# A hybrid attention, state-space and spectral-filter kernel: the filter loop gets its own buffers, and its matrices and frequencies are dealt out by stride

## The chip, the cores and the metric

The kernel runs on one core of one Trainium2 chip, in float32. The metric is the time of one execution on the device in microseconds (us). A core has a matrix engine (TensorE, PE in the profile), VectorE (DVE), ScalarE (ACT), GpSimd (POOL) and SyncE (SP, which here issues nearly all DMAs, in order). TensorE reads its operands from SBUF and writes PSUM, 8 banks of 2 KB for each of 128 rows. "Eviction" means the copy of a PSUM result to SBUF by VectorE or ScalarE.

## What is computed

Input `x` is 8 images of 32 x 32 tokens with 128 channels. Three residual layers follow each other, softmax attention with 4 heads, a state-space layer run forward and backward, and a spectral filter over 1024 tokens an image:

```python
x = x + _L0_conv_ref(_gn(x), L0_conv_w_qkv, L0_conv_w_out, L0_conv_b_out)
t = _to_tokens(x)
t = t + _L1_attn_ref(_ln_t(t), L1_attn_fwd_in_proj, ...)
t = t + _L1_ffn_ref(_ln_t(t), L1_ffn_sigma, L1_ffn_phi, ...)
```

The change touches the last one. For tokens u, 16 filters phi and one of four banks of matrices, chosen by the weights:

```python
Vf = jnp.fft.rfft(phi, n=n, axis=0)
Uf_p = jnp.fft.rfft(u, n=n, axis=1)
Uf_m = jnp.fft.rfft(u * sgn3, n=n, axis=1)
U_plus = jnp.fft.irfft(Vf[None, :, :, None] * Uf_p[:, :, None, :], n=n, axis=1)[:, :sl]
U_minus = jnp.fft.irfft(Vf[None, :, :, None] * Uf_m[:, :, None, :], n=n, axis=1)[:, :sl]
out = jnp.einsum('btkd,k,kde->bte', U_plus, s, Mpp)
out = out + jnp.einsum('btkd,k,kde->bte', U_minus, s, Mpm)
```

To this comes a short regression over three shifted copies of u. The kernel does not filter and then multiply by the matrices; for each frequency it first sums the 16 matrices with the filters' spectra as weights, and then multiplies the token spectra by that one matrix.

## The kernel before

The part up to about 930 us (attention and most of the state-space layer) is not touched. Then come three stages, all inside `fast_kernel`:

1. *The end of the state-space stage* (lines 1448 to 1545), with all engines and SP in an order written by hand. Here batches 0 and 1 already get their token spectra, and the last lines add the state-space output to X[7], store it to `xd`, load it back in another layout (`reload(u)`, line 1542) and store the residual of batch 1 to `xa` (`store_residual(1)`).
2. *The spectra loop* (lines 1558 to 1625; b from 2 to 8). For each batch, `transform(b)` turns the normalized tokens (8 transposes `cpt`, line 561), forms their spectra (16 matmuls `pf`, line 571; the additions that finish them run on VectorE and GpSimd), stores them to DRAM (`store_spectra`, to `ud`, 1 MB) and copies the turned tokens to `ut`. `taps_of(b - 1, k)` does the regression of the batch before (matmuls `pu`, line 601, in two halves) and adds it to X; then X goes to `xa`. Between the halves, in b = 2 to 5, `turned(n)` takes a quarter (bank) of the 32 matrices from DRAM (`md`, eight matrices in a row), transposes them (`mdt`, line 1573), copies them to `me` in SBUF (line 1574) and stores them to DRAM `me` (line 1577). After the fourth bank, four DMAs of 512 KB (line 1580) spread all of `me` into `mst`: 32 rows for each of four groups, a row for each matrix.
3. *The filter loop* (lines 1629 to 1744). The 128 frequencies go in 16 chunks of 8. For a chunk, `matrices(c, n, gs)` is called for n = 0 to 7: 16 small matmuls `pg` (line 1644) into four one-bank PSUM tiles, evicted in turn by ScalarE (line 1657) and VectorE (line 1655) to `gs`, 64 KB a row. `loaded_spectra(c)` brings the chunk's spectra `u` from `ud` and GpSimd makes a second, turned copy (lines 1667 and 1668). `apply` multiplies (`py`, line 1678), `gather` combines the results and stores them to `yd` (line 1701). Chunk c + 1 gets its matrices while chunk c is applied, two calls and one quarter of `apply` in alternation; the first chunk's matrices come alone. `fetch(c)` (line 1709) brings a part of chunk c's results back as rows of `early_yt`. After the loop the rest is loaded (line 1753), and the inverse transform `pz` (line 1769) and the last additions give the output.

In the spectra loop PE, DVE, ACT and POOL keep the program's order and SP's order is the scheduler's; in the filter loop likewise. Buffers come from pools that are opened and closed as a stack, on two sides of SBUF. The filter loop's pool `g_2` holds two `gs` and two `u`; it opens where the spectra loop's pools and the pool `resid` with all X[b] have just been closed (`middle.close()`), so it lies on the places that these had. Whoever first writes such a place waits for all that still uses it. The PSUM pools change at the same point: in the spectra loop `ps_f` has two tiles of two banks, `ps_o` two of one, `ps_t` one of two; in the filter loop `ps_g` has eight of one.

Of the kernel before, what the change touches and what calls it, by code (L numbers as in the profile page):

```python
# [14 lines left out]
P = 128  # L15
B = 8
# [29 lines left out]
def fast_kernel(ctx: ExitStack, tc: tile.TileContext, a: dict, out: bass.AP, bad: bass.AP):  # L46
# [29 lines left out]
    me = dram.tile([P, 2 * KF, P], F32, name="me")  # L76
# [243 lines left out]
    def transforms(pool, tables):  # L320
# [5 lines left out]
        odd = counted(pool, [2, NF], [[512, 2], [2, NF]], 1, 0, "odd")  # L326
# [31 lines left out]
    def transform_taps(pool, ps, tables):  # L358
# [34 lines left out]
        alt = pool.tile([P, NF // 2, 2], F32, name="alt")  # L393
        nc.gpsimd.memset(alt, 1.0)
        nc.gpsimd.memset(alt[:, :, 1], -1.0)
        alt = alt.rearrange("p f i -> p (f i)")
# [533 lines left out]
    with ExitStack() as s:  # L930
# [611 lines left out]
        reload(u)  # L1542
# [10 lines left out]
    with ExitStack() as s:  # L1553
        mp = s.enter_context(tc.tile_pool(name="c_m", bufs=1, side="right"))
        mst = mp.tile([P, 32, C], F32, tag="mst", name="mst")
        early_yt = mp.tile([P, 2, 4, 4, C], F32, name="early_yt")

        with ExitStack() as s2:
            p1 = s2.enter_context(tc.tile_pool(name="f_1", bufs=1))
            p2 = s2.enter_context(tc.tile_pool(name="f_2", bufs=2))  # L1560
            ps_f = s2.enter_context(tc.tile_pool(name="f_ps_f", bufs=2, space=PSUM))
# [3 lines left out]
            def turned(n, pool, tag, size):  # L1565

                t = p2.tile([P, 8, C], F32, tag="md", name=f"md{n}")
                nc.sync.dma_start(t, md.rearrange("d r k e -> d (r k) e")[:, n * 8 : n * 8 + 8, :])
                to = p2.tile([P, 8, C], F32, tag="me", name=f"me{n}")
                for at in range(0, 8, size):  # L1570
                    pt = pool.tile([P, size, C], F32, tag=tag, name=f"mdt{n}_{at}")
                    for i in range(size):
                        nc.tensor.transpose(pt[:, i, :], t[:, at + i, :], ident)  # L1573
                    nc.vector.tensor_copy(
                        to[:, at : at + size].rearrange("p k d -> p (k d)"), pt.rearrange("p k d -> p (k d)")
                    )
                nc.sync.dma_start(me[:, n * 8 : n * 8 + 8, :], to)
                if n == 3:
                    for g in range(4):
                        nc.sync.dma_start(  # L1580
                            mst[g * 32 : (g + 1) * 32],
                            me[g * 32 : (g + 1) * 32].rearrange("n k d -> k n d"),
                        )
# [23 lines left out]
            s2.enter_context(tc.manual_schedule(engines=IN_ORDER))  # L1607
            uts = {}
            for _ in scaled(3, *third, p2):
                pass  # L1610
            for b in range(2, B + 1):
                if b + 2 < B:
                    norms[b + 2] = normalize(p2, b + 2)
                if b < B:
                    transform(b)
                if 3 < b + 1 < B:
                    for _ in normalized(b + 1, p2, *norms.pop(b + 1), wide=p2):
                        pass
                if b > 2:
                    taps_of(b - 1, 0)  # L1620
                if 2 <= b <= 5:
                    turned(b - 2, *((ps_o, "o", 4) if b == 2 else (ps_t, "t", 8)))
                if b > 2:
                    taps_of(b - 1, 1)
                    store_residual(b - 1)
        middle.close()
        middle.close()

        with ExitStack() as s2:
            p2 = s2.enter_context(tc.tile_pool(name="g_2", bufs=2))  # L1630
            p3 = s2.enter_context(tc.tile_pool(name="g_3", bufs=3))
            ps_g = s2.enter_context(tc.tile_pool(name="g_ps_g", bufs=8, space=PSUM))

            turn = 0

            def matrices(c, n, gs):

                nonlocal turn
                pts = [ps_g.tile([P, 4, P], F32, tag="g", name=f"pg{c}_{n}_{g}") for g in range(4)]
                cols = slice(c * FC, (c + 1) * FC)  # L1640
                for e in range(4):
                    for g in range(4):
# [948 lines left out]
```

## Time and profile before

| what | value |
|---|---|
| median of 3 runs | 1395.06 us (1393.53, 1395.06, 1397.17) |
| profiled execution, its own time | 1403.45 us |
| its span, first to last instruction | 1401.6 us |
| mean granted TensorE clock | 0.980 |
| TensorE busy | 1330.1 us, 95% of the span |
| VectorE, ScalarE, GpSimd busy | 79%, 66%, 38% |
| spectra loop | about 999 to 1069 us |
| entry to the filter loop (no `py` yet) | 1069 to 1088 us |
| filter loop with `py` | 1088 to 1356 us |
| tail | 1357 to 1402 us |

A row of the timeline reads: start in the span, duration, engine, line, operation, tile written <- tiles read, shapes, count of instructions merged; in brackets the time that the engine sat idle before it, and what released it. "SPq" is the issue of a DMA by SP; its duration is that of the issue, not of the transfer. "issue" as a releaser means that the engine waited for nothing that the profile shows. The granted clock is TensorE's, as a share of full speed.

In the filter loop with `py` TensorE is busy for 246.5 of 252.4 us (stretch 1088.4 to 1340.8), at clock 1.00 and a DMA share of 0.27.

### The profile page before, as it was taken

To read this page: it belongs to the slowest core of one execution; us is meant where nothing else is said; L and a number is where in the kernel's file an instruction comes from. 1 tells how busy PE (TensorE), PEld (TensorE's weight loads), DVE (VectorE), ACT (ScalarE), POOL (GpSimd) and SP (SyncE) were. 2 spreads that over 40 slices of the span, in tenths; PEclk is the share of its full clock that TensorE was granted. 3 is DMA by queue.
4 is the path that set the end of the run, shared out by engine and by line. 5 is a ranking of instruction groups with operands and counts; after the bars stand their busy time and mean duration, and the time that the engine had idled before them with its cause. 6 is when DMAs were issued, how large, how long until landed. Compare 5 with 4: busy or idle time off the path is not lost. (4 is left out here: it accounts for less than half of the span.)

```text
span 1401.6 us, 47569 instructions
## 1 busy us (share of the span) xinstructions
PE 1330.1 (95%) x20926; PEld 844.7 (60%) x20926; DVE 1103.4 (79%) x2145; ACT 922.8 (66%) x1428; POOL 536.0 (38%) x510
## 2 busy tenths in 40 slices
PE   7999999999999999999999999998898999999967
PEld 4333333333333666666666666667797988888964
DVE  5789888788778688988889898999564777777745
ACT  5666666766756888888878888876353555555520
POOL 3412986876910343434343343444673011111100
PEclk9999999999999999999999999999999999999979
DMA  7100111111101434444444343431668132222357
GB/s 172 55 2 2 38 39 39 53 39 39 31 1 42 96 78 93 108 94 113 94 108 94 92 95 88 114 83 48 197 208 198 46 78 73 77 69 70 83 171 294
DMA packets 139391, 123.24 MB, mean 88 GB/s; under 512 B 44808, under 2 KB 118152, under 8 KB 135080
## 3 DMA queue, kind: packets, MB, share of 16 engines
q1 hardware_dynamic: 137048, 115.93, 32.0%
q8 instruction: 166, 2.72, 0.8%
q10 hardware_dynamic: 2128, 4.19, 0.8%
q14 instruction: 49, 0.40, 0.1%
HBM read 78.15 MB, written 34.08 MB: 80 GB/s over the span
## 5 line engine op out<-in xcount | busy, mean ns | idle before, releaser
L809 ACT ACTIVATE pr<-pt 128x1024 f32<-128x1024 f32 x256 | 248.2, 1022 | 105.0 <-PE pt L804 103.9
L1657 ACT COPY gs<-pg 128x512 f32<-128x512 f32 x256 | 133.1, 603 | 75.6 <-PE pg L1644 58.4
L1655 DVE COPY gs<-pg 128x512 f32<-128x512 f32 x256 | 159.1, 685 | 26.0 <-PE pg L1644 18.9
L834 DVE TENSOR_TENSOR two<-pr,pr 128x1024 f32<-128x1024 f32 x128 | 164.8, 1328 | 15.2 <-ACT pr L809 15.2
L804 PE MATMUL pt<-q,k 32*128 32x512 f32 x1024 | 162.5, 651 | 6.1 <-ACT pr L809 4.1
L1644 PE MATMUL pg<-taps,mst 32*128 32x128 f32 x4096 | 150.1, 283 | 11.9 <-issue 5.8
L1644 PEld LDWEIGHTS pg<-taps,mst 32*128 32x128 f32 x4096 | 135.0, 189 | 27.2 <-issue 19.3
L825 PE MATMUL po<-pr,v 128*32 128x512 f32 x1024 | 140.6, 610 | 0.0
L1678 PE MATMUL py<-gs,u 128*32 128x128 f32 (+1 forms) x4096 | 130.9, 281 | 3.4 <-issue 3.4
L1030 POOL TENSOR_TENSOR ec<-ec,ct 128x2048 f32<-128x2048 f32 x16 | 83.6, 5224 | 112.3 <-ACT ct L1110 57.1
L1072 DVE SCALAR_TENSOR_TENSOR xs<-xp,cw,xs 128x1024 f32<-128x1024 f32 x96 | 122.5, 1283 | 2.2 <-issue 0.2
L1678 PEld LDWEIGHTS py<-gs,u 128*32 128x32 f32 (+1 forms) x4096 | 114.8, 141 | 10.9 <-issue 3.6
L1094 PE MATMUL pb<-bxt,wbc 128*128 128x512 f32 x256 | 114.0, 597 | 3.6 <-ACT zs L1085 3.6
L1667 POOL TENSOR_SCALAR u<-u 128x512 f32<-128x512 f32 x16 | 24.0, 1499 | 237.5 <-DMA u<-ud 138.3
L804 PEld LDWEIGHTS pt<-q,k 32*128 32x128 f32 x1024 | 49.5, 185 | 88.9 <-ACT pr L809 27.1
L1193 DVE SCALAR_TENSOR_TENSOR state<-state,dec,pst 128x64 f32<-128x64 f32 x448 | 87.3, 275 | 1.1
L1302 POOL TENSOR_TENSOR rms<-rms_v,mhalf 128x8 f32<-128x8 f32 x16 | 26.5, 1659 | 157.0 <-DVE rms_v L1300 157.0
L1094 PEld LDWEIGHTS pb<-bxt,wbc 128*128 128x128 f32 x256 | 47.1, 189 | 60.3 <-issue 55.0
L825 PEld LDWEIGHTS po<-pr,v 128*32 128x32 f32 x1024 | 27.8, 110 | 89.7 <-issue 86.4
L1016 POOL TENSOR_TENSOR lm<-cs,lm 128x2048 f32<-128x2048 f32 x16 | 57.9, 3620 | 57.7 <-DVE xs L1072 22.6
L845 PE MATMUL pd<-two,ones 128*32 128x512 f32 x512 | 74.1, 618 | 2.3 <-DVE two L834 2.1
L1272 PEld LDWEIGHTS spo<-wo,y 128*128 128x128 f32 x512 | 62.1, 191 | 13.1 <-issue 8.9
(310 smaller groups left out, 2784.5 us busy)
## 6 DMA issues: line engine op xcount, KB each, us to landing
lm<-cd SPq DMA_DIRECT2D x32, 512.0 KB
ec<-cd SPq DMA_DIRECT2D x32, 512.0 KB
ud<-sp SPq DMA_DIRECT2D x8, 1024.0 KB
u<-ud SPq DMA_DIRECT2D x32, 256.0 KB
yd<-sums SPq DMA_DIRECT2D x32, 256.0 KB
moved<-state SPq DMA_DIRECT2D x48, 128.0 KB
room<-yd SPq DMA_DIRECT2D x6, 1024.0 KB
X<-in_x SPq DMA_DIRECT2D x8, 512.0 KB
```

The costliest lines, as they stand in the source:

```text
L804: nc.tensor.matmul(pt[:, i, :], lhsT=k[rows, j * P : (j + 1) * P], rhs=q[rows, cols], start=True, stop=True)
L809: nc.scalar.activation(pr[:, 2 * g : 2 * g + 2, :].rearrange("p i t -> p (i t)"), pt.rearrange("p i t -> p (i t)"), AF.Exp, scale=SCALE,)
L825: nc.tensor.matmul(po[rows, :], lhsT=vs[b][:, j, rows], rhs=pr[:, h, :], start=(j == 0), stop=(j == NT - 1))
L834: nc.vector.tensor_tensor(two, sums["pr"][:, 2 * g : 2 * g + 2, :], pr[:, 2 * g : 2 * g + 2, :], ALU.add)
L1030: t = nc.gpsimd.tensor_tensor(u.ec, u.ec, u.ct.unsqueeze(1).to_broadcast([P, NH, NT, L]), ALU.mult)
L1072: u.convolved = nc.vector.scalar_tensor_tensor(acc, xp[:, at : at + T], cw[u.d][:, n, i : i + 1], acc, ALU.mult, ALU.add)
L1094: nc.tensor.matmul(u.pb[:, i * 512 : (i + 1) * 512], lhsT=wbc[u.d][:, k, :], rhs=xt[:, at : at + 512], start=(k == 0), stop=(k == KC - 1),)
L1193: nc.vector.scalar_tensor_tensor(u.state[:, k, h, :], u.state[:, k - 1, h, :], u.dec[:, c, h, j : j + 1], u.pst[c][:, j, h, :], ALU.mult, ...
L1644: nc.tensor.matmul(pts[g][:, e, :], lhsT=mst[rows, n * 4 + e, :], rhs=taps[rows, cols].rearrange("p f q m i -> p (f q m i)"), start=True, ...
L1655: nc.vector.tensor_copy(to, frm)
L1657: nc.scalar.copy(to, frm)
L1678: nc.tensor.matmul(py[t * 32 : t * 32 + 32 - 16 * m, q // 2, :], lhsT=u[:, i, m:, :, :, q * FC + f].rearrange("p k b i -> p (k b i)"), rhs ...
```

## The change

- The matrices are dealt out by stride. `me` is laid out as four banks of eight; bank n takes the matrices n, n + 4, n + 8 and so on, so it is loaded from `md` in runs of 512 bytes. Each bank is spread to `mst` by four DMAs of its own, `spread(n)`, at the start of b = 4, 5, 6 and 7: 8 rows each, every fourth row of a group. So 16 DMAs of 128 KB take the place of 4 of 512 KB.
- `turned(n)` moves from b = 2 to 5 to b = 3 to 6. All banks have buffers from a pool of three (`f_m`); banks 0 to 2 are asked for ahead of the loop, bank 3 in `turned(0)`. The first bank no longer uses the half-size PSUM tiles of `ps_o`.
- `reload(u)` of X[7] moves behind the load of bank 0; with that, `store_residual(1)` stands ahead of it on SP. SP is in hand-written order in the spectra loop.
- `gs` and `u` of even chunks come from a pool `c_g` that opens ahead of the spectra loop, on the other side of SBUF; those of odd chunks from a pool `g_g` on the old place. `early_yt` is taken later.
- Two of the eight calls of `matrices` for chunk 0 move into the last pass of the spectra loop (b = 8), one between the two halves of batch 7's regression, one after them, with two `ps_f` tiles each. `u` of chunk 0 is loaded at the end of that loop.
- Chunk c now has the frequencies c, c + 16, c + 32, ...: the tables `odd` and `alt` are permuted, `yd` is written four separate frequencies at a time, and `fetch` fills rows of `early_yt` that are 16 apart.

```diff
-    me = dram.tile([P, 2 * KF, P], F32, name="me")
+    me = dram.tile([P, 4, KF // 2, P], F32, name="me")
...
-        odd = counted(pool, [2, NF], [[512, 2], [2, NF]], 1, 0, "odd")
+        odd = counted(pool, [2, NF // FC, FC], [[512, 2], [2, NF // FC], [2 * NF // FC, FC]], 1, 0, "odd")
+        odd = odd.rearrange("p i c f -> p i (c f)")
...
-        alt = pool.tile([P, NF // 2, 2], F32, name="alt")
+        alt = pool.tile([P, NF // FC // 2, 2, FC], F32, name="alt")
...
         add_rows(u)
-        reload(u)
         for k in range(NB):
             add_taps(1, k, po[:, k])
         store_residual(1)
...
-        early_yt = mp.tile([P, 2, 4, 4, C], F32, name="early_yt")
+        first_gs = s.enter_context(tc.tile_pool(name="c_g", bufs=1, side="right"))
...
-                t = p2.tile([P, 8, C], F32, tag="md", name=f"md{n}")
-                nc.sync.dma_start(t, md.rearrange("d r k e -> d (r k) e")[:, n * 8 : n * 8 + 8, :])
+            def load_bank(n):
+                mds[n] = pm.tile([P, 8, C], F32, tag="md", name=f"md{n}")
+                nc.sync.dma_start(mds[n], md.rearrange("d r k e -> d (r k) e")[:, n::4, :])
+
+            def turned(n):
+
+                if n == 0:
+                    load_bank(3)
+                pt = ps_t.tile([P, 8, C], F32, tag="t", name=f"mdt{n}")
+                for i in range(8):
+                    nc.tensor.transpose(pt[:, i, :], mds[n][:, i, :], ident)
                 to = p2.tile([P, 8, C], F32, tag="me", name=f"me{n}")
...
-                nc.sync.dma_start(me[:, n * 8 : n * 8 + 8, :], to)
-                if n == 3:
-                    for g in range(4):
-                        nc.sync.dma_start(
-                            mst[g * 32 : (g + 1) * 32],
-                            me[g * 32 : (g + 1) * 32].rearrange("n k d -> k n d"),
-                        )
+                nc.vector.tensor_copy(to.rearrange("p k d -> p (k d)"), pt.rearrange("p k d -> p (k d)"))
+                nc.sync.dma_start(me[:, n], to)
+
+            def spread(n):
+                for g in range(4):
+                    nc.sync.dma_start(
+                        mst[g * 32 + n : (g + 1) * 32 : 4],
+                        me[g * 32 : (g + 1) * 32, n].rearrange("n k d -> k n d"),
+                    )
...
-            s2.enter_context(tc.manual_schedule(engines=IN_ORDER))
-            uts = {}
-            for _ in scaled(3, *third, p2):
+            s2.enter_context(tc.manual_schedule(engines=ALL_IN_ORDER))
+            uts, mds = {}, {}
+            for n in range(3):
+                load_bank(n)
+                if n == 0:
+                    reload(units[-1])
+            gs, begun = {0: chunk_matrices(0, first_gs)}, set()
+
+            def double_banks(n):
+                pts = [ps_f.tile([P, 2, 4, P], F32, tag="f", name=f"pg0_{n}_{i}") for i in range(2)]
+                begun.add((-1, n))
+                matrices(0, n, gs[0], [pts[g // 2][:, g % 2] for g in range(4)])
+
+            def ahead(b, place):
+                for _ in range(planned.get((b, place), 0)):
+                    double_banks(len(begun))
+
+            planned = {(B, 1): 1, (B, 2): 1}
+            for _ in scaled(3, *third, px):
                 pass
             for b in range(2, B + 1):
+                if 4 <= b <= 7:
+                    spread(b - 4)
...
+                ahead(b, 0)
                 if b > 2:
                     taps_of(b - 1, 0)
-                if 2 <= b <= 5:
-                    turned(b - 2, *((ps_o, "o", 4) if b == 2 else (ps_t, "t", 8)))
+                ahead(b, 1)
+                if 3 <= b <= 6:
+                    turned(b - 3)
                 if b > 2:
                     taps_of(b - 1, 1)
                     store_residual(b - 1)
+                ahead(b, 2)
+            us = {0: loaded_spectra(0, first_gs)}
...
+            second_gs = s2.enter_context(tc.tile_pool(name="g_g", bufs=1))
+            yp = s2.enter_context(tc.tile_pool(name="g_y", bufs=1, side="right"))
+            early_yt = yp.tile([P, 2, 4, 4, C], F32, name="early_yt")
...
-                at = c * FC + n * 4
+                at = c + n * 4 * chunks
                 nc.sync.dma_start(
-                    yd[at : at + 4].rearrange("f k b i q e -> (f k b i) (q e)"), sums.rearrange("p q e -> p (q e)")
+                    yd[at :: chunks][:4].rearrange("f k b i q e -> f (k b i) (q e)"), sums.rearrange("p q e -> p (q e)")
                 )
...
-                rows = slice(c * FC, (c + 1) * FC)
+                rows = slice(c, NF, chunks)
...
                 if c + 1 < chunks:
-                    gs[c + 1] = p2.tile([P, P, C], F32, tag="gs", name=f"gs{c + 1}")
-                    us[c + 1] = loaded_spectra(c + 1)
+                    if c >= 0:
+                        gs[c + 1] = chunk_matrices(c + 1, second_gs if c % 2 == 0 else first_gs)
+                        us[c + 1] = loaded_spectra(c + 1, second_gs if c % 2 == 0 else first_gs)
...
-                        matrices(c + 1, 2 * n, gs[c + 1])
-                        matrices(c + 1, 2 * n + 1, gs[c + 1])
+                        for i in range(2 * n, 2 * n + 2):
+                            if (c, i) not in begun:
+                                matrices(c + 1, i, gs[c + 1], single_banks(c + 1, i))
```

## The prediction

> **What bounds the kernel now.** I read the page's busy shares first, then the table of stretches, then the chain of waits in order of time and the timeline around each pause of TensorE. TensorE is busy for 95% of the span, so only its pauses, its slow stretches and the tail can be won. The change touches what lies after about 999 us. From the table of stretches, spectra loop and filter loop (columns: start:end, length, busy time of each engine with the number of instructions, granted TensorE clock, DMA share, GB/s):
>
> ```profile
> 995.00:1010.00 15.00, 9.17 (x58) 8.22 (x57) 7.32 (x25) 5.34 (x12) 11.38 (x21) 0.90 0.70 204
> 1010.00:1022.50 12.50, 12.50 (x82) 11.73 (x81) 7.39 (x24) 5.34 (x12) 8.02 (x15) 0.84 0.65 218
> 1022.50:1033.10 10.60, 10.60 (x83) 10.19 (x82) 7.76 (x24) 5.34 (x12) 7.52 (x15) 1.00 0.76 249
> ...
> 1069.00:1088.40 19.40, 14.02 (x320) 13.51 (x320) 11.21 (x19) 9.54 (x19) 4.08 (x4) 0.82 0.54 141
> ```
>
> The second and third lines are the same work for two batches: 12.5 us at clock 0.84, 10.6 at 1.00. Two pauses stand before the slow lines. Timeline, with the idle time of the engine and its releaser in brackets:
>
> ```profile
> 1003.40 1.09 ACT L566 COPY ut<-cpt 128x512 f32<-128x512 f32 x2
> 1008.00 1.94 PE L1573 MATMUL mdt<-ident,md 128*128 128x128 f32 x8 [5.11 <-DMA md<-md]
> 1009.73 1.91 PE L561 MATMUL cpt<-ident,ln_x 128*128 128x128 f32 x8
> ...
> 1044.13 0.37 SPq L592 DMA_DIRECT2D ud<-sp  x1
> 1044.61 1.81 SPq L1577 DMA_DIRECT2D me<-me  x1
> 1050.90 4.57 SPq L1580 DMA_DIRECT2D mst<-me  x4
> ...
> 1069.22 2.07 PE L1644 MATMUL pg<-taps,mst 32*128 32x128 f32 x64 [0.84 <-DVE X L611]
> 1075.81 2.05 ACT L1657 COPY gs<-pg 128x512 f32<-128x512 f32 x4 [16.49 <-DMA xa<-X]
> 1075.92 2.49 DVE L1655 COPY gs<-pg 128x512 f32<-128x512 f32 x4 [6.75 <-DMA xa<-X]
> 1082.42 7.27 DVE L1655 COPY gs<-pg 128x512 f32<-128x512 f32 x12 [0.42 <-PE pg L1644]
> 1088.43 2.02 PE L1678 MATMUL py<-gs,u 128*32 128x128 f32 x64
> ```
>
> The first pause is a wait for the first turned bank, 5.11 us. The second: eight PSUM banks are full after 2.07 us, and no eviction may start because `gs0` lies where X[7] is still being stored. The chain of waits shows that store, and at the end of the loop two transfers that stand on the path:
>
> ```profile
> 1069.60 5.75 DMA xa<-X
> ...
> 1357.57 2.40 DMA yd<-sums
> 1359.99 3.53 DMA early_yt<-yd
> ```
>
> **What the Trainium skill says.** (1) "DMA: Bandwidth & Descriptors", section "Why a DMA increments its semaphore by 16 and not by 1": a DMA runs on the largest number of engines up to 16 that divides the outermost sizes of both sides. The new spreads have 8 rows, the new `yd` stores have 4 on one side, so 8 and 4 engines where 16 worked. No row of before shows such a store. (2) "SBUF — State Buffer", section "Door 1: The DMA port swizzle (why `[64,N]` ≈ `[32,N]`)": 32 rows in a row reach half the ports, 189 GB/s at 1 MiB. The trace agrees: the spread of `mst` filled 1052 to 1063 at 188 GB/s. (3) "TensorE: Matmul & The Clock Gate", Part 1: after some 3.4 us of idleness the clock halves until about 3.4 us of work have passed. The trace agrees: a pause of over 5 us stands before each of the stretches at 0.84 and 0.82, and 1009 to 1011 shows 0.50.
>
> **Part one, start of the spectra loop.** `turned(0)` moves from batch 2 to batch 3, its bank is asked for before the loop, and store_residual(1) now stands between bank 0 and the reload of X[7]. The next TensorE work after 1002.9 is then transform(3), which needs the two copies of `ut`, done at 1004.49, and `ln_x`, done earlier. It starts near 1004.6, not 1009.73: -5.1 us. Batch 3 then runs warm: from its first transpose to batch 4's took 12.8 us (1009.73 to 1022.53), the two batches after it 10.56 each; I take 10.6, so -2.2 (ends 0 and -2.2). Bank 0 must be there at 1004.6 + 0.87 + 3.46 + 2.68 = 1011.6; in 512-byte pieces it takes 1.9 us (0.52 MB at 281 GB/s, the rate of the `ud` stores in 1023 to 1027, whose runs are 512 bytes), behind `ud` and `xd` at about 1009.5: covered. `turned(3)` now stands in batch 6, which had none: 8 transposes, +0.9. Sum -6.4. VectorE loses two half copies of 0.69 and gains a whole one of 1.22; GpSimd needs some 8 us of each 10.6: both hidden.
>
> **Part two, entry to the filter loop.** Before: from the last `pu` (1068.38) to the first `py` (1088.43) 20.05 us. After, `gs0` has a place of its own, so the store of X[7] holds nothing until `gs1`. The built program gives this order on TensorE: pu(7,0), a call of matrices, pu(7,1), a second call, six more. A call is 1.04 us (half of 2.07). The two early calls share PSUM tiles in pairs, and the built waits show VectorE's eviction held until ScalarE's of the same tile is done, and call three held until VectorE's last: 0.59 + 0.68 + 0.68 + about 0.1 = 2.1 us. Then 1.04 for call three and twelve evictions on VectorE. The pace is from before: sixteen took 1075.92 to 1082.42 + 8 x 0.606 = 1087.27, 0.71 each; twelve, 8.5. From the sixteenth to `py` 1.16. Sum, leaving out pu(7,1), which both have: 1.04 + 1.04 + 2.1 + 1.04 + 8.5 + 1.16 = 14.9, so -5.2, less a wait s.
>
> The wait s is what the change adds: the early calls read every fourth matrix of all four spreads, and pu(7,1), the store of X[7] and `u0` stand behind them. The last spread: batch 6 starts at 1004.6 + 3 x 10.6 = 1036.4; `ud` of a batch is issued 11.05 us after it (1033.09 to 1044.13), so 1047.4; from there to the landing of `me` was 6.8 us (1044.13 to 1050.90), so SP issues the spread at 1054.2. With 8 engines at 281/16 GB/s, 141 GB/s, it takes 3.7 us, plus about 1 us at each end (taken from the last `xa`: the DMA share fell to 0.24 in 1073 to 1074 and 0.06 in 1074 to 1075, ScalarE went on at 1075.81): 1059.9. It is needed at 1047.0 + 0.87 + 3.46 + 5.36 + 2.68 = 1059.4. But the queue is nearly full: from 999 to 1059 six `ud` of 3.7, eleven half-megabyte transfers of 1.3 (400 GB/s in 1049 to 1051), four banks of 1.9 and four spreads of 3.7 make 58.9 us of 60, with SP standing in order before each spread for its `me`. The idle half of the engines during a spread helps. I take s = 1.5, ends 0 and 5. Part two: -3.7.
>
> Hidden here: sixteen spread issues on SP in place of four (some 0.8 us each, covered by the engines' 10.6 us per batch; where not, that is s); `u0`, issued after the store of X[7] near 1066 and ready 7.6 us later as before (1075.61 to 1083.2), some 4 us ahead of `py`; `gs1`'s wait for the same store, landed near 1068, used near 1077.
>
> **Part three, loop and tail.** In the loop the `yd` stores on 4 engines take about 2.6 us each where 0.65 did (0.26 MB at 400 GB/s, times 16/4); two to a chunk of 16.5 us, at a DMA share of 0.30: hidden. The last store is on the path: +2.0 (ends 0 and 2). The fetch to rows sixteen apart reaches four ports where eight rows in a row reach two (place 2 above); the two fetches of 1109.0 to 1110.5 ran at 98 GB/s, so I take -0.8 (ends 0 and -1). Net +1.2. The permuted tables (`odd`, `alt`) have equal sizes: nothing.
>
> **Sum.** -6.4 - 3.7 + 1.2 = -8.9 us. On the profiled execution of 1403.45 us (span 1401.6 and 1.85 around it) that is 1394.5. It was 8.4 us above the median of the three runs, 1395.06; I carry the difference over: 1386.2. The ends together: best -6.4 - 5.2 - 1 = -12.6, worst -4.2 - 0.2 + 2 = -2.4, so 1382.5 to 1392.7; the runs scatter by 1.8 around the middle.
>
> **Rivals.** *Late spreads*: the wait moves from X[7] to `mst`, s of 5 to 8. For it: the count of 58.9 of 60 us; against it: spreads fill gaps in which the queue stood still (a DMA share of 0.01 in 1019 to 1022). Then about -3.5: 1391.5. *The entry stays as long*: some other wait (evictions held in pairs, `u0`, `gs1`) takes all of part two. For it: each of the first twelve evictions has a new companion; against it: each wait is shorter than the 5.75 us it replaces. Then -6.4 + 1.2 = -5.2: 1389.9. *Spreads so slow that the kernel is slower*: four in series on one in-order queue, so each further microsecond of a spread is paid four times. With s = 1.5 + 4 x (spread - 3.7) the gain is gone at s = 10.4 (5.9 us a spread) and the kernel is slower by over 4 us from 7.0 us a spread, 75 GB/s. At 7.5 us, s = 16.7 and the change is +6.3: 1401.4. For it: half the engines, each with one row; against it: 141 GB/s by the same packets elsewhere. *The change doesn't do what it says* (bank 0 still late) gives back the 7.3 of part one: -1.6, 1393.5, counted with late spreads.
>
> **How the numbers follow.** Forecast 0.70, late spreads 0.15, entry as long 0.09, slower 0.06. A difference of 0.3%, 4.2 us, is about what a measurement of this kernel tells from no change. Faster by more (below 1390.9): nearly all of the first, 0.4 of the second, 0.7 of the third: 0.81; slower 0.06; the same 0.13. Range: the ends, the scatter, and most of the second case: 1381.5 to 1392.5.
>
> **What would show it.** Right: no TensorE pause over 2 us near 1003; 1.00 in the stretch of batch 3; the first `py` near 1079; a pause of 0 to 5 us before the first `pg`, released by `mst`; a last `yd` store of over 4 us in the chain. Wrong: a longer pause before `pg`, transposes of batch 3 waiting for `md`, or `py` still near 1088.

## The result, and the profile after

The changed kernel takes 1400.1 us (median of 22 runs, 1392.97 to 1405.22), the kernel before, run beside it, 1398.21 us (22 runs, 1392.96 to 1403.21). The ratio is 1.0012 with a 95% interval of 0.9999 to 1.0025: no change, or up to 3.5 us slower. Forecast were 8.9 us less. The profiled execution has a span of 1398.5 us at a mean clock of 0.984 (before: 1401.6 at 0.980); it took 1400.27 us, close to its kernel's median.

The table of stretches of the changed kernel, for the places that were shown of before (start:end, length, busy time of PE, PEld, DVE, ACT and POOL with instructions, granted TensorE clock, DMA share, GB/s):

```profile
995.00:1010.00 15.00, 12.62 (x83) 11.30 (x83) 9.93 (x42) 6.55 (x17) 11.91 (x22) 1.00 0.63 180
1010.00:1022.50 12.50, 12.50 (x97) 12.03 (x96) 8.96 (x27) 6.58 (x15) 11.59 (x23) 1.00 0.86 261
1022.50:1033.10 10.60, 10.60 (x82) 10.19 (x82) 7.81 (x25) 5.37 (x13) 8.02 (x16) 1.00 0.76 241
...
1055.00:1069.00 14.00, 10.24 (x86) 9.05 (x85) 2.25 (x3) 0.58 (x2) 3.75 (x8) 0.85 0.82 270
```

The clock of 0.84 behind 1010 is gone: the start of the spectra loop runs warm. The low clock and the idle TensorE stand now in 1055 to 1069, which was at 1.00 before. The timeline of the changed kernel shows why:

```profile
1006.05 1.09 PE L562 MATMUL cpt<-ident,ln_x 128*128 128x128 f32 x8 [1.66 <-ACT ut L567]
...
1049.83 2.80 SPq L1622 DMA_DIRECT2D mst<-me  x4
1052.74 0.41 SPq L593 DMA_DIRECT2D ud<-sp  x1
1053.25 3.48 SPq L1618 DMA_DIRECT2D me<-me  x1
...
1060.47 2.80 SPq L1622 DMA_DIRECT2D mst<-me  x4
1063.39 0.48 PE L1581 MATMUL pg<-taps,mst 32*128 32x128 f32 x2 [2.51 <-DMA mst<-me]
...
1064.96 3.82 PE L1581 MATMUL pg<-taps,mst 32*128 32x128 f32 x30 [1.09 <-DMA mst<-me]
1068.70 4.26 PE L602 MATMUL pu<-m_u,ut 128*128 128x128 f32 x24
...
1085.71 2.02 PE L1711 MATMUL py<-gs,u 128*32 128x128 f32 x64
```

Read SP's lines first. The four transfers that spread bank 2 are issued at 1049.83, because SP stood there for bank 2's store (`me`) to land; only then come `ud` and, at 1053.25, the store of bank 3. That store has to land before bank 3's own spread, which is issued at 1060.47. Batch 7 began at 1048.35, so the last spread is issued 12.1 us after it. TensorE has reached the first early call of `matrices` (tile `pg`) near 1060.9 and waits, first 2.51 us, then in shorter pieces; the second half of the last regression, which stands behind this call, starts at 1068.70 and takes 4.26 us for 24 matmuls where 2.84 are usual. The tail of the changed kernel:

```profile
1349.40 0.54 SPq L1734 DMA_DIRECT2D yd<-sums  x1
1349.98 6.93 SPq L1742 DMA_DIRECT2D early_yt<-yd  x3
1356.96 2.34 SPq L1788 DMA_DIRECT2D gs<-yd  x4
1358.33 5.31 PE L1804 MATMUL pz<-early_yt,inv 128*128 128x512 f32 x8 [10.24 <-DMA early_yt<-yd]
...
1384.20 1.67 PE L1804 MATMUL pz<-gs,inv 128*128 128x256 f32 x6 [2.96 <-SPq L2596]
```

The same place before, where the last store was issued at 1357.57:

```profile
1357.94 2.67 SPq L1709 DMA_DIRECT2D early_yt<-yd  x3
1360.66 2.22 SPq L1753 DMA_DIRECT2D room<-yd  x4
1363.87 6.18 PE L1769 MATMUL pz<-early_yt,inv 128*128 128x512 f32 x8 [7.60 <-DMA early_yt<-yd]
```

SP stood with the fetches for 6.93 us (2.67 before), since they wait for the last `yd` store. The loads of the other three quarters (`gs<-yd`, before `room<-yd`) stand behind them in the same queue: they are issued 7.56 us after the last store instead of 3.09. At 1384.20 TensorE goes on after another pause, of 2.96 us. It is put down to line 2596 on SP, the branch on a flag at the end of the program, which these matmuls do not need. The matmuls behind the pause read the last of these loads, and the kernel with the dealing alone names that load (below, "The tail").

### The profile page after: what moved, and what is told of

Read it like the earlier page. It is cut to its first block, busy times and chain, and to the rows that moved or that the text cites. A ratio compares the mean times of both kernels' runs of the same rounds, so it can differ in the third digit from the quotient of the medians.

```text
span 1398.5 us, 47581 instructions
## 1 busy us (share of the span) xinstructions
PE 1325.5 (95%) x20926; PEld 841.6 (60%) x20926; DVE 1105.9 (79%) x2144; ACT 922.0 (66%) x1428; POOL 537.4 (38%) x510
## 5 line engine op out<-in xcount | busy, mean ns | idle before, releaser
L835 DVE TENSOR_TENSOR two<-pr,pr 128x1024 f32<-128x1024 f32 x128 | 164.1, 1322 | 13.4 <-ACT pr L810 13.0
L805 PEld LDWEIGHTS pt<-q,k 32*128 32x128 f32 x1024 | 49.5, 185 | 88.3 <-ACT pr L810 27.0
L1017 POOL TENSOR_TENSOR lm<-cs,lm 128x2048 f32<-128x2048 f32 x16 | 57.9, 3620 | 57.7 <-DVE xs L1073 34.7
```

What stands on the lines that cost most here:

```text
L805: nc.tensor.matmul(pt[:, i, :], lhsT=k[rows, j * P : (j + 1) * P], rhs=q[rows, cols], start=True, stop=True)
L835: nc.vector.tensor_tensor(two, sums["pr"][:, 2 * g : 2 * g + 2, :], pr[:, 2 * g : 2 * g + 2, :], ALU.add)
```

## The experiments

Every kernel was timed in five rounds beside the kernel before (the one repeat of before in one round), and profiled once. All ratios are to the kernel before, as it ran in the same rounds. Where two edited kernels are compared by their ratios, the difference is uncertain by some 3 us, an estimate from the widths of the two intervals. The stretches are differences of starts in the timelines: from the first `cpt` of batch 2 to that of batch 7 (start of the spectra loop), from there to the first `py` (entry), and from the last chunk's first `py` to the end (tail), in us.

| kernel | start | entry | tail | ratio (95%) |
|---|---|---|---|---|
| before | 55.7 | 35.3 | 60.8 | 1 |
| before, profiled again | 55.5 | 35.2 | 58.4 | 0.9991 (0.9972 to 1.0010) |
| changed | 49.4 | 37.4 | 63.1 | 1.0012 (0.9999 to 1.0025) |
| before, banks ahead | 49.4 | 40.5 | 58.8 | 1.0009 (0.9986 to 1.0033) |
| ... last two banks in batch 5, one after the other | 51.0 | 35.1 | 58.8 | 0.9996 (0.9976 to 1.0015) |
| ... last two banks in batch 5, apart | 51.4 | 33.5 | 57.9 | 0.9962 (0.9947 to 0.9976) |
| before, frequencies dealt | 55.8 | 35.1 | 63.8 | 1.0030 (1.0012 to 1.0049) |
| changed, no early calls | 49.4 | 30.6 | 61.5 | 0.9952 (0.9935 to 0.9969) |
| changed, spread behind the next store | 49.4 | 34.0 | 61.9 | 0.9983 (0.9967 to 0.9998) |
| changed, last two banks in batch 5 | 51.3 | 29.2 | 61.0 | 0.9961 (0.9944 to 0.9978) |
| changed, one transfer a bank | 49.4 | 31.2 | 63.0 | 0.9945 (0.9921 to 0.9968) |
| changed, frequencies in a row | 49.4 | 37.1 | 57.6 | 0.9985 (0.9968 to 1.0003) |
| changed, `yd` store in four | 49.4 | 38.2 | 61.2 | 1.0004 (0.9987 to 1.0022) |
| in a row, one transfer a bank | 49.4 | 30.9 | 58.6 | 0.9923 (0.9896 to 0.9951) |
| ... and last two banks in batch 5 | 51.0 | 29.2 | 58.1 | 0.9930 (0.9906 to 0.9954) |
| ... and no early calls instead | 49.4 | 28.1 | 58.5 | 0.9904 (0.9876 to 0.9931) |

What is not in the table scatters from profile to profile without a visible order by edit: batch 2 starts between 994.6 and 1000.2 us in the sixteen profiles, and the loop from the first `py` to the last chunk's takes 248.5 to 257.6 us.

### Part one alone

All edits are shown shortened; `...` and the words behind `#` are not in the code. This one also puts SP into the hand-written order of the change.

```
-        reload(u)                      # end of the state-space stage
...
+    for n in range(3):                 # ahead of the spectra loop
+        load_bank(n)
+        if n == 0:
+            reload(units[-1])
...
+    if b == 7: spread()                # one spread of all banks, ahead of batch 7's spectra
-    if 2 <= b <= 5: turned(b - 2, ...)
+    if 3 <= b <= 6: turned(b - 3)
```

> The kernel before with the change's first part alone: three turned banks asked for ahead of the spectra loop, their transposes in batches 3 to 6 instead of 2 to 5, SP in the written order, one spread of whole groups after the last bank. Theory A (the start of the loop gained what was forecast, the entry and the tail gave it back): 5 to 7 us under the kernel before (ratio 0.995 to 0.9965), no TensorE pause over 2 us near 1003, batch 3 at clock 1.00. Theory B (the profiled execution of before was an unlucky one, and in most executions the pause cost less): 0 to 3 us under it. Theory C (the last bank, turned one batch later, makes the single spread late for the filter loop): not under it, with a pause before the first pg that mst releases.

1399.3 us, ratio 1.0009 (0.9986 to 1.0033). The start is 6.2 us shorter and the entry 5.3 us longer. Timeline of this kernel:

```profile
1052.65 4.59 SPq L1581 DMA_DIRECT2D mst<-me  x4
...
1060.90 0.49 PE L1651 MATMUL pg<-taps,mst 32*128 32x128 f32 x4 [0.84 <-DVE X L611]
1063.53 0.79 PE L1651 MATMUL pg<-taps,mst 32*128 32x128 f32 x2 [2.14 <-DMA mst<-me]
1066.09 3.68 PE L1651 MATMUL pg<-taps,mst 32*128 32x128 f32 x58 [1.77 <-DMA mst<-me]
```

The single spread (on 16 engines, where those of the change have 8; these counts are the prediction's, no view of the runs lists a transfer's engines) was in time in the kernel before and is late now: its last bank comes a batch later, and the batches come earlier. This is theory C. Whether the gain exists when the spread is not late was tried with the last two banks turned in batch 5:

```
-    if b == 7: spread()
+    if b == 6: spread()
-    if 3 <= b <= 6: turned(b - 3)
+    if 3 <= b <= 5: turned(b - 3)
     ...
+    if b == 5: turned(3)               # after the second half of the taps
```

> As the kernel before with banks ahead (the first experiment), but the last two banks are both turned in batch 5, so that the single spread is issued one batch earlier, ahead of batch 6's spectra. Theory C (the first part's gain of 6 us was lost again because the last bank, a batch later, made the spread late for the filter loop): batch 7's first transpose to the first py falls back from 40.5 to about 35.2 us, the value of before, where the store of X[7] rules; 5 to 7 us under the kernel before (ratio 0.995 to 0.9965). Rival (the first part's gain is lost elsewhere): not under the kernel before by more than 2 us.

The entry fell to 35.1 us, as theory C has it, but the time did not: ratio 0.9996 (0.9976 to 1.0015). Part of the gap is plain: the next batch's `cpt` waits 1.41 us for the copy of bank 3 out of the one PSUM tile that both use, and start and entry together are 4.7 us shorter, not 6. The rest was open. So the same was tried with bank 2 turned ahead of the first half of the taps and bank 3 between the halves:

```
+    if b == 5: turned(2)               # before the first half
-    if 3 <= b <= 5: turned(b - 3)
+    if 3 <= b <= 5: turned(3 if b == 5 else b - 3)
-    if b == 5: turned(3)
```

> The kernel before with banks ahead, the last two turned in batch 5 on both sides of the first half of the taps, so that neither the pause of 1.4 us nor the late spread of the two earlier variants is left. Theory C: batch 2's first transpose to batch 7's falls from 55.6 to 49.5 us and batch 7's to the first py stays 35.2: 6 us under the kernel before, ratio 0.994 to 0.9975. If the time is still that of the kernel before while these two stretches of its trace are as said, then the first part's gain is lost outside the stretch between batch 2 and the first py.

1392.56 us, ratio 0.9962 (0.9947 to 0.9976), 5.3 us less, with start and entry together 6.0 us shorter (to the mean of the two profiles of before). They share it otherwise than expected: the start is 51.4 us, not 49.5, since bank 2's transposes now wait 1.71 us for ScalarE to empty the same PSUM tile, and the entry is 33.5, not 35.2. In this kernel the gain of part one reaches the end. The wait for the store of X[7] stands at the entry again, as before (TensorE waits for ScalarE's copy, which waits for that store, `xa`):

```profile
1065.75 2.07 PE L1653 MATMUL pg<-taps,mst 32*128 32x128 f32 x64 [0.84 <-DVE X L611]
1071.90 11.38 PE L1653 MATMUL pg<-taps,mst 32*128 32x128 f32 x256 [4.08 <-ACT gs L1666]
```

The stretches of these two variants differ by only 1.2 us, their ratios by 4.7 us. Why the first of them did not come nearer to the 4.7 us that its stretches show (0.6 measured, at most 3.4) stays open, and so the gain at the end is shown by one of two kernels.

> The kernel before, profiled once more. If its batch 3 shows the pause near 1003 but runs at clock 1.00 behind it, the 2.2 us of the forecast for a slow batch 3 was an accident of one execution; if it shows a pause of 5 us and a clock of about 0.84 again, the term stands and the gain of the first part was lost later.

In the second profile of before, the pause is there again, 5.21 us, and the batch behind it is again slow (in the second line, a stretch, the clock is the third number from the end):

```profile
1006.51 1.94 PE L1573 MATMUL mdt<-ident,md 128*128 128x128 f32 x8 [5.21 <-DMA md<-md]
...
1008.20:1020.50 12.30, 12.30 (x82) 11.63 (x81) 7.54 (x25) 5.34 (x12) 8.05 (x15) 0.86 0.65 219
```

So the forecast's term for a slow batch 3 was no accident of one execution.

### The entry: early calls, order of the queue, engines of the spread

```
-planned = {(B, 1): 1, (B, 2): 1}
+planned = {}
```

> The changed kernel without its two calls of matrices inside the spectra loop; all eight stand in the filter loop. Theory A (the wait for mst stalls pu(7,1), the store of X[7], u0 and the clock behind it): the first pg starts at the landing of the spread, near 1066, with pu(7,1) done before; sixteen evictions of 0.71 us and 1.2 us more give the first py near 1079 instead of 1085.7: 4 to 7 us under the changed kernel, so 2 to 5 under the kernel before. Rival (the evictions and u0 set the entry, the early calls do save their 2 us): equal to the changed kernel or 2 us over it.

1390.91 us, 0.9952 (0.9935 to 0.9969), by the ratios some 8 us under the changed kernel where 4 to 7 were expected. The first `py` comes at 1079.44, as expected. TensorE's timeline of this kernel:

```profile
1053.19 10.88 PE L602 MATMUL pu<-m_u,ut 128*128 128x128 f32 x96
1064.91 1.26 PE L1581 MATMUL pg<-taps,mst 32*128 32x128 f32 x6 [0.84 <-DVE X L612]
1066.58 12.94 PE L1581 MATMUL pg<-taps,mst 32*128 32x128 f32 x314 [0.41 <-DMA mst<-me]
```

The last spread is nearly as late as in the changed kernel (issued 11.6 us after batch 7's start), but all of the regression runs meanwhile, and 0.41 us is left of the wait. So the early calls stood where the wait does harm: other work that was ready stood behind them. Then the two possible reasons for the late spread were tried. First the order of SP's queue, with the spreads still on 8 engines:

```
-    if 4 <= b <= 7: spread(b - 4)      # first in the batch
+    if b == 7: spread(3)
...
     if 3 <= b <= 6: turned(b - 3)
+    if 4 <= b <= 6: spread(b - 4)
```

> The changed kernel with the same spreads on 8 engines, but the spreads of banks 0, 1 and 2 stand behind the next bank's store in SP's order instead of ahead of it. Theory Q (SP's order: the spread of one bank, standing for its store to land, holds back the store of the next bank, so the last spread is issued 4 to 5 us later than its data allow): the last me store is issued near 1 us after batch 7's first transpose instead of 4.9, the last spread 8 us after it instead of 12.1, the pauses before the first pg fall below 1.5 us, and the kernel is 4 to 6 us under the changed one (ratio to before 0.9955 to 0.9985). Rival W (8 engines instead of 16 make the spreads late): the pauses stay, the time within 1.5 us of the changed kernel.

1396.71 us, 0.9983 (0.9967 to 0.9998). Its timeline, with batch 7 from 1049.62:

```profile
1049.99 2.70 SPq L1618 DMA_DIRECT2D me<-me  x1
1052.75 3.49 SPq L1622 DMA_DIRECT2D mst<-me  x4
...
1057.67 2.78 SPq L1622 DMA_DIRECT2D mst<-me  x4
...
1062.73 0.48 PE L1581 MATMUL pg<-taps,mst 32*128 32x128 f32 x2 [0.58 <-DMA mst<-me]
1063.60 0.48 PE L1581 MATMUL pg<-taps,mst 32*128 32x128 f32 x2 [0.38 <-DMA mst<-me]
1064.47 0.48 PE L1581 MATMUL pg<-taps,mst 32*128 32x128 f32 x2 [0.39 <-DMA mst<-me]
1065.28 2.00 PE L1581 MATMUL pg<-taps,mst 32*128 32x128 f32 x26 [0.32 <-DMA mst<-me]
1067.21 3.69 PE L602 MATMUL pu<-m_u,ut 128*128 128x128 f32 x24
```

The last bank's store is issued 0.4 us after batch 7's start and its spread 8.05 us after it, as theory Q says; the entry is 3.4 us shorter. By the ratios the kernel is some 4 us under the changed one, the lower end of what was expected. What is left are four short waits, some 0.85 us apart, as many as the spread has transfers, and a slow clock behind them: from the issue of the spread to the end of the last wait are 7.6 us. Next the transfers, with the spreads at their old place in the order:

```
-me = dram.tile([P, 4, KF // 2, P], F32, name="me")
+me = dram.tile([4, 4, KF // 2, 32, P], F32, name="me")
-nc.sync.dma_start(me[:, n], to)
+for g in range(4):
+    nc.sync.dma_start(me[n, g].rearrange("k n d -> n k d"), to[g * 32 : (g + 1) * 32])
-for g in range(4): nc.sync.dma_start(mst[g * 32 + n : (g + 1) * 32 : 4], ...)
+nc.sync.dma_start(mst[n::4].rearrange("r n d -> r (n d)"), me[n].rearrange("g k n d -> (g k) (n d)"))
```

> The changed kernel with me laid out in DRAM so that a bank is spread by one transfer of 32 rows of 16 KB (16 engines) instead of four of 8 rows (8 engines); the bank is stored by four transfers of 32 rows instead of one. Theory A (the half-used engines make the spreads late): the last spread lands 3 us earlier, the pause before the first pg falls from 6.8 to about 3 us: 3 to 5 us under the changed kernel. Rival (what is late is the bank's own store and the in-order queue ahead of it): the pause stays over 5 us, the time within 1.5 us of the changed kernel.

```profile
1053.51 0.45 SPq L1622 DMA_DIRECT2D mst<-me  x1
...
1057.69 1.17 PE L1581 MATMUL pg<-taps,mst 32*128 32x128 f32 x32 [1.20 <-DMA mst<-me]
```

1391.45 us, 0.9945 (0.9921 to 0.9968), some 9 us under the changed kernel where 3 to 5 were expected. One wait of 1.20 us is left, and the regression's second half takes 2.94 us. This edit shortens the queue too (the last spread is issued 9.55 us after batch 7's start, not 12.1). But that is 1.5 us later than in the kernel with the spread behind the next store (8.05), and yet the entry is 2.8 us shorter (31.2 against 34.0): from the issue to the end of the wait are 4.2 us instead of 7.6. So rival W has a part too: when the last spread comes late, four transfers on 8 engines reach TensorE later than one on 16. Whether the engines, the number of transfers or the traffic beside them does it, no run separates. The next kernel keeps the four transfers on 8 engines and the dealt frequencies, but turns the last two banks in batch 5:

```
-    if 4 <= b <= 7: spread(b - 4)
+    if 4 <= b <= 6: spread(b - 4)
+    if b == 6: spread(3)
+    if b == 5: turned(2)               # before the first half of the taps
-    if 3 <= b <= 6: turned(b - 3)
+    if 3 <= b <= 5: turned(3 if b == 5 else b - 3)
```

> The changed kernel with its dealt frequencies and its spreads on 8 engines, but with the last two banks both turned in batch 5 and their spreads in batch 6. If only the lateness of the last spread cost the entry (and not the 8 engines as such): no pause before the first pg, first py 29 to 30 us after batch 7's first transpose instead of 37.4, so 6 to 8 us under the changed kernel, ratio to before 0.9945 to 0.9975. If the spreads on 8 engines are slow in themselves, a pause of over 2 us before the first pg stays and it is under 4 us better.

```profile
1047.16 6.45 SPq L1622 DMA_DIRECT2D mst<-me  x8
...
1060.85 1.17 PE L1581 MATMUL pg<-taps,mst 32*128 32x128 f32 x32
1061.95 2.95 PE L602 MATMUL pu<-m_u,ut 128*128 128x128 f32 x24
...
1077.63 2.01 PE L1715 MATMUL py<-gs,u 128*32 128x128 f32 x64
```

1393.02 us, 0.9961 (0.9944 to 0.9978), some 7 us under the changed kernel. No wait is left and the entry is 29.2 us, the same as with one transfer a bank and the last two banks in batch 5. When the last spread is issued early enough, the 8 engines cost nothing.

### The tail

The dealing of the frequencies taken out of the changed kernel, with its permuted tables `odd` and `alt`:

```
-at = c + n * 4 * chunks
+at = c * FC + n * 4
-yd[at :: chunks][:4].rearrange("f k b i q e -> f (k b i) (q e)"), ...
+yd[at : at + 4].rearrange("f k b i q e -> (f k b i) (q e)"), ...
-rows = slice(c, NF, chunks)
+rows = slice(c * FC, (c + 1) * FC)
```

> The changed kernel with its frequencies in a row again: old tables, a chunk of eight neighbouring frequencies, yd stores on rows in a row, fetches of eight rows in a row. Theory A (the last yd store on few engines and its fetch cost 2.6 us at the tail): last yd issue to pz back from 8.9 to about 6.3 us, 2 to 4 us under the changed kernel. Rival (the tail's difference is chance or the pause near 1381): no difference, within 1 us.

1397.51 us, 0.9985 (0.9968 to 1.0003), by the ratios some 4 us under the changed kernel, the upper end of what was expected. From the issue of the last store to the first load of the other quarters there are 3.06 us again (1345.86 to 1348.92). The mirror of it, the same lines the other way round put alone into the kernel before:

> The kernel before with the frequencies dealt out alone: tables, yd stores of 4 x 32 rows, fetches of rows sixteen apart. Theory T (the tail pays for the last store, for its fetch and for the transfers behind them): TensorE's pause before the first pz 10.2 to 10.6 us instead of 7.6, and a further pause of 1 to 3 us in the last quarter of the tail: 3 to 5 us over the kernel before (ratio 1.002 to 1.0035). As forecast (1.2 us): 1.0009. Rival (the dealing helps the loop by its fetches to more ports): not over the kernel before.

1405.39 us, 1.0030 (1.0012 to 1.0049): 4.2 us slower, 1.7 to 6.9, as theory T has it. SP and TensorE in its tail:

```profile
1355.47 0.53 SPq L1702 DMA_DIRECT2D yd<-sums  x1
1356.05 7.04 SPq L1710 DMA_DIRECT2D early_yt<-yd  x3
1363.14 2.37 SPq L1754 DMA_DIRECT2D room<-yd  x4
1364.70 5.34 PE L1770 MATMUL pz<-early_yt,inv 128*128 128x512 f32 x8 [10.53 <-DMA early_yt<-yd]
...
1390.58 1.61 PE L1770 MATMUL pz<-room,inv 128*128 128x256 f32 x6 [2.94 <-DMA room<-yd]
```

The same picture as in the changed kernel: 7.67 us from the last store to the loads, and both pauses; here the second is put down to the loads by name. The chain of waits shows the last store, 6.38 us where the chain of before had 2.40, and the last of the loads ahead of the end:

```profile
1355.47 6.38 DMA yd<-sums
...
1370.42 20.12 DMA room<-yd
```

To part store and fetch, the store was made in four transfers of 32 rows in a row, with the fetch as changed:

```
...
+for t in range(4):
+    nc.sync.dma_start(yd[at + t * chunks]..., sums[t * 32 : t * 32 + 32]...)
```

> The changed kernel with every yd store issued as four transfers of 32 rows in a row, one for each frequency, in place of one transfer on 4 x 32 rows. Theory E (the store on 4 engines is what is slow at the tail): TensorE's pause before the first pz falls from 10.2 to 8 to 9 us (three more issues of some 0.4 us each take part of it back); 1 to 2 us under the changed kernel. Theory F (the fetch of rows sixteen apart is slow): the pause stays at 10 us or more.

```profile
1354.74 2.65 SPq L1744 DMA_DIRECT2D early_yt<-yd  x4
1357.44 2.30 SPq L1790 DMA_DIRECT2D gs<-yd  x4
...
1359.03 2.90 PE L1806 MATMUL pz<-early_yt,inv 128*128 128x512 f32 x3 [7.34 <-DMA early_yt<-yd]
```

TensorE's pause is 7.34 us instead of 10.24, even less than theory E expected, and the fetches are as quick as in the kernel before (2.65 us on SP). So the slow part is the store. Of the 4.5 us by which the loads stood further behind the end of the last `py` (8.87 us against 4.39), 3.1 come back (5.75). The pause in the last quarter is still there (2.98 us). The tail is 1.9 us shorter than the changed kernel's, but in the time this does not show: 1399.95 us, 1.0004 (0.9987 to 1.0022), where 1 to 2 us were expected.

### Together

> The changed kernel with both the frequencies in a row and the spread of a bank as one transfer of 32 rows. If the two costs add (entry 6, tail 4 to 5 us): 10 us under the changed kernel, near 1388 (ratio to before 0.992 to 0.9945). If one hides the other: as the better of the two alone, 1391.

1389.12 us, 0.9923 (0.9896 to 0.9951), 10.8 us under the kernel before: entry and tail add. To this the last two banks in batch 5 were added:

> The changed kernel with frequencies in a row, a bank's spread as one transfer, and the last two banks turned in batch 5, their spreads in batch 6. Then no pause is left before the first pg (1.5 us with the last bank in batch 6): first py about 29.3 us after batch 7's first transpose instead of 30.85; 1 to 2 us under the kernel without that step, ratio to before about 0.991. Rival (the spreads now crowd with the spectra's stores): no gain or a loss of up to 2 us.

1387.61 us, 0.9930 (0.9906 to 0.9954). There is no gain of 1 to 2 us. The entry is 29.2 us as expected, 1.6 us less, but the start is 1.6 us more, since a pause of 1.41 us for the single PSUM tile of the transposes comes with it. The last kernel has the early calls taken out instead:

> The changed kernel with frequencies in a row, a bank's spread as one transfer, and without the two early calls of matrices. If the early calls are worth nothing even where mst is nearly in time (their saving of 1 us a call goes into the third call's wait of 2 us for their evictions): within 1.5 us of the kernel with both edits and the early calls, ratio to before about 0.992. If they are worth their place: 2 us over it, 0.9935.

1385.75 us, 0.9904 (0.9876 to 0.9931): the lowest of all, 13.4 us under the kernel before, though its interval overlaps with those of the last two. Its entry of 28.1 us is also shorter than the 29.2 us with early calls that wait for nothing. TensorE's timeline at this entry:

```profile
1061.55 12.15 PE L1580 MATMUL pg<-taps,mst 32*128 32x128 f32 x320 [0.84 <-DVE X L611]
1073.63 2.02 PE L1707 MATMUL py<-gs,u 128*32 128x128 f32 x64
```

## Why the prediction was wrong

**Part one: right in the stretch it named.** Forecast -6.4 us; the start is 49.40 us instead of 55.73 and 55.48, -6.2. Batch 2 to 3 takes 7.10 us instead of 12.29, -5.2 (forecast -5.1). Batch 3 takes 10.62 instead of 12.63, -2.0 (forecast -2.2, with batch 4's first transpose read at 1022.53 where the timeline has 1022.36). The three batches up to batch 7 take 31.68 instead of 30.81, +0.9 as forecast. That this counts to the end is shown by the kernel with this part alone and the banks apart (-5.3 us), but not by the other variant whose spread is in time.

**Part two: the step that failed is the wait s.** What the change removes was right: -5.2 us without a wait were forecast, and with the wait gone the entry is 29.2 us instead of 35.2, -6.0. But s was taken as 1.5 us, at most 5. The prediction put the issue of the last spread at 7.2 us after batch 7's start, by adding, from batch 6's start, 11.05 us to `ud` and 6.8 us from there to the landing of `me`. Both were read in the kernel before, in whose queue no spread stands between them. In the changed kernel the spread of bank 2 waits there for bank 2's store, ahead of `ud` and of bank 3's store, and the issue is at 12.1 us. The order alone is the cause of most of this: with the spread behind the next store it is at 8.05 us. That SP stands in order before each spread was written in the count of 58.9 of 60 us, but only as a full queue, not as a chain in which each bank's store waits for the spread of the bank before.

The transfer was priced near enough for the changed kernel: 5.7 us from issue to use were forecast, and the first wait is over 2.9 us after the issue, the last, near 1066.7, 6.2 us after it. With the order changed it was 7.6 us, with one transfer on 16 engines 4.2. That the idle half of the engines helps is shown by no run. From the end of the regression's first half to the start of its second are 7.8 us, 1.04 of them the call: s is 6.8 us. What stands behind the wait was named, but not its clock: the second half took 1.4 us longer. With the measured -6.0, -6.0 + 6.8 + 1.4 = +2.2; the entry shows +2.1 instead of -3.7.

**The early calls** were the part of the change that made the wait dear. Even where nothing is late they lose about 1.1 us in the profiles (29.2 against 28.1 us). The third call waits 2.00 us for their evictions, as forecast; without them VectorE's sixteen evictions, begun only after the regression, are done sooner all the same.

**Part three: a term of the sum mis-sized, and a path left out.** Forecast +1.2 us, of it +2.0 for the store. The tail is 61.0 to 63.8 us in the six kernels with dealt frequencies and one store, 57.6 to 60.8 in the nine with frequencies in a row, on the mean 3.8 us apart; alone, the dealing cost 4.2 us (1.7 to 6.9). The last store takes 4.0 us more, not 2.0 (6.38 against 2.40 in the chains of waits), and SP issues the loads behind it 4.5 us later (7.56 us after it against 3.09). The fetch then takes 1.8 us less (1.42 us from the end of its last issue to the first `pz` against 3.26), not 0.8: +2.7 at the first `pz`. TensorE's pause there is 10.2 to 10.6 us in all six and 7.0 to 7.6 in all nine.

There the sum ended: it priced the fetch, but not the loads of the other three quarters behind it in the queue. The profile of before hid them, for TensorE did not wait for them in it; in its second profile it waits 1.45 us. In every kernel in which TensorE waits for the last of these loads, whatever its store, the wait ends 25.7 to 27.8 us after the first of them was issued. So when the loads are issued later the end comes later, less what slack TensorE had. This pause is not a clean mark of the dealing: 0.6 to 3.0 us in the six, 0 to 2.1 in the nine. From the first `pz` to the end are 38.7 us on the mean of the six and 37.6 on that of the nine, +1.1. In the loop no price of the stores shows above the scatter.

**The sum.** -6.2 + 2.1 + 3.5 (the tail's 63.1 against the mean 59.6 of the two profiles of before) = -0.6 us, for +1.7 (-0.1 to 3.5) measured. The remaining 2 us are not explained, and may be more than scatter: twelve of the thirteen kernels with the new start take longer than their three stretches add up to, by 2.3 us on the mean of the thirteen (-0.9 to 5.0), while the dealing alone, with the old start, agrees to 0.1 us. Part of the start's gain may be lost outside the stretches; the loop, which scatters by 9 us between single profiles, hides where. Of the 13.9 us between the forecast of 1386.2 and the 1400.1 measured, 3.2 come from the base: 1395.06 was the median of three runs, 1398.21 that of 22.

**The rivals.** *Late spreads*, forecast with a chance of 0.15 and 1391.5 us, is what happened at the entry: s of 5 to 8, a pause that `mst` releases. It gave too good a time since it took the tail as in the sum and left out the clock. *The entry stays as long* is near by its number only: evictions, `u0` and `gs1` were not the reason, as the entry of 29.2 us without the wait shows. *Spreads so slow that the kernel is slower* had the queue in series right and named too much of the cause: the transfer took 6.2 us from issue to use, near the forecast, and the kernel on 8 engines with earlier banks has no wait at all. *The change doesn't do what it says* did not happen: no transpose waited for `md`.

**The signs.** No pause over 2 us near 1003, a warm batch 3 and, in the chain of the dealing alone, a last `yd` store of over 4 us came true. The first `py` came near 1086 instead of 1079. The pause before the first `pg`, 2.51 us, lay within the 0 to 5 us of the sign for a right forecast, because the wait came in pieces: a sign on the first pause did not measure s.

## What to carry to other kernels

When a store and the load that needs it go through one queue in order, find each wait in the queue's new order before adding intervals from the old trace: whatever stands behind the waiting load, the next store above all, moves with it, and store, landing and load of one piece delay those of the next. Work put ahead of its place does harm if its data come late and other work stands behind it; put it where everything that is ready has been done. At the end of a kernel, price a slower store by the last transfer that stands behind it, not only by the first use. And take more than one profile of the kernel before: a wait that is absent from one may be in the next.

## What was not expected of the hardware

The clock fell without any long pause. In the kernel with the spread behind the next store, no wait between 1062 and 1067.2 was longer than 0.58 us, and the granted clock of this stretch was 0.83 and of the next 0.79 (table of stretches of that kernel):

```profile
1062.00:1067.20 5.20, 3.52 (x34) 2.58 (x32) 0.75 (x1) 0.28 (x1) 0.00 (x0) 0.83 1.03 317
1067.20:1071.00 3.80, 3.80 (x29) 3.67 (x32) 1.35 (x3) 0.79 (x2) 0.00 (x0) 0.79 0.18 67
```

TensorE was busy for 3.52 of 5.20 us there. The Trainium skill, "TensorE: Matmul & The Clock Gate", Part 1, says that the gate is set by how busy TensorE has been recently; this agrees. So several short waits for one tile can cost the clock too, here four of 1.7 us together; one wait of 1.20 us, in the kernel with one transfer a bank, left it at 1.00.

The issue on SP has a price of its own: a `yd` store on 4 x 32 rows took 0.54 us to issue where one on 128 rows took 0.33. For a bank's store it is not a matter of the form alone: as one transfer it took 1.6 us for the first bank and 3.4 to 3.5 for the others in the changed kernel, and 1.4 to 2.7 with the spread behind it. Why is open.
